# Two token tiles at a time in the down projection: seven products of quarters in place of eight

## The chip, the cores and the metric

The kernel runs on one core of a Trainium2 chip. The metric is device time in microseconds, the median of several executions. One further execution was recorded by the hardware profiler; the lines of profile in this document come from it. The engines are named PE (TensorE; PEld is its weight load), DVE (VectorE), ACT (ScalarE), POOL (GpSimd) and SP (SyncE, which here issues all the DMAs).

## The reference

1024 tokens of width 512 (two sequences of 512) go through four residual layers: a block-sparse linear layer, a gated FFN, a state-space mixer, and the same FFN with the same weights again. Each begins with a layer norm. The FFN, which is what the change touches:

```python
gate_proj = dequantize(gate_w, gate_s, gate_z, GROUP_SIZE, dt)   # 512 x 1792
up_proj = dequantize(up_w, up_s, up_z, GROUP_SIZE, dt)           # 512 x 1792
down_proj = dequantize(down_w, down_s, down_z, GROUP_SIZE, dt)   # 1792 x 512
gate = jax.nn.silu(jnp.dot(x, gate_proj))
up = jnp.dot(x, up_proj)
return jnp.dot(gate * up, down_proj)
```

`dequantize` subtracts a zero and multiplies by a scale, per group of 128 rows and per column. All is float32.

## The kernel before

Tokens come in eight tiles of 128 (`NT`), the width in four chunks of 128 (`KC`), the inner width 1792 in 14 chunks of 128 (`NFC`) or seven slabs of 256 (`NSLAB`). The residual stream `x_sb` stays in SBUF, tokens on the partitions; `xn_t` is the normed input, transposed. `h_t` holds silu(gate) * up transposed, inner width on the partitions, and `down` the dequantised down weights.

`ffn(which, first, waiting, after)` is called for both FFNs. Slab 0's gate and up products are plain (L417). From slab 1 on, each of the gate and up products of a slab is made by `seven` (L169): both the weights and the tokens are cut in two in both directions, and seven products of quarters replace eight (Strassen's scheme in Winograd's form). `seven` is a generator which the caller advances product by product, so that other work can be put between. Its seven products run in PSUM banks of tag `proj` for gate and `yo` for up, three banks each; the right-hand sums stand in `tq`, the left-hand ones are made on POOL by `left_sides` (L163 to L166). The sums of products are taken on DVE (L192, L197, L198, L206, L211), the gate's silu on ACT (L441) and the gating on DVE (L445). `tmp` is a ring of three SBUF tiles: for sums in the up product, and for normed tiles (`room`).

In each slab, the next slab's gate and up weights and this slab's down weights are dequantised (`dequant`, L225 to L231): three DMAs into `wi`, `zi`, `sf` (two buffers each), a subtraction on DVE (L230), and a product on POOL (L231). The down weights of slab s come behind five of the seven products of its up matrix:

```python
for _ in range(3):
    next(u)
dequant_down(s)
```

When all slabs are done, the down projection runs tile by tile, 14 matmuls of 128x128 by 128x512 each in one bank of tag `proj`, then an addition into `x_sb` on DVE (L474) and the callback `after(t, sg_tile)`. For the second FFN `after` stores the tile. For the first it is `to_mixer`: it stores the tile in DRAM (`x_d`), loads weights for the mixer, has the normed tile from two tiles ago transposed (`turn`, L134, with the copy to `xn_t` on ACT, L135), norms this tile (`norm`, L107 to L121), and for t = 5 begins the mixer's step sizes of the first sequence (`step_sizes`, `pd` on PE at L521), whose rest runs at t = 6 (L534 to L542).

Then the mixer begins: cumulated step sizes (`decays`: `pacs`, `pa`, `pl` on PE, which read `acs`), the last two tiles turned, the sums `two_quarters` (L145, L146) on DVE and `third_quarter`, `last_quarter` (L149, L156) on POOL, and the first products of `seven`.

The instructions of PE, ACT and DVE run in the order in which the program writes them. POOL and SP have their instructions ordered by a scheduler.

Of the kernel before, what the change touches and what calls it, by code (L numbers as in the profile page):

```python
# [8 lines left out]
F32 = mybir.dt.float32  # L9
# [5 lines left out]
P = 128  # L15
NTOK = 1024
NT = NTOK // P
SEQ = 512
NCH = SEQ // P
DIM = 512  # L20
KC = DIM // P
KH = KC // 2
# [7 lines left out]
NFC = FF // P  # L30
SLAB = 256
NSLAB = FF // SLAB
# [5 lines left out]
def kernel(  # L38
# [25 lines left out]
    nc = tc.nc  # L64
# [5 lines left out]
    psum = ctx.enter_context(tc.tile_pool(name="psum", bufs=2, space=bass.MemoryType.PSUM))  # L70


    x_sb = keep.tile([P, NT, DIM], F32, name="x_sb")
    xn_t = keep.tile([P, KC, NTOK], F32, name="xn_t")

    tq = keep.tile([P, 3, KH, SEQ], F32, name="tq")

    def room(*_):
        return keep.tile([P, SEQ], F32, tag="tmp", name="tmp", bufs=3)

    def weights():
# [10 lines left out]
        out=tri, in_=tri, compare_op=ALU.is_ge, fill=0.0, base=0, pattern=[[1, P]], channel_multiplier=-1  # L92
# [58 lines left out]
    def quarters():  # L151
        two_quarters()
        third_quarter()

    def last_quarter():
        nc.gpsimd.tensor_sub(B12, B22, B12)  # L156

    def left_sides(w):

        a11, a12, a21, a22 = w[:, :KH, 0], w[:, KH:, 0], w[:, :KH, 1], w[:, KH:, 1]  # L160
        sq = keep.tile([P, 3, KH, P], F32, tag="ws", name="ws", bufs=3)
        s1, s2, s4 = sq[:, 0], sq[:, 1], sq[:, 2]
        nc.gpsimd.tensor_add(s1, a21, a22)  # L163
        nc.gpsimd.tensor_sub(a21, a11, a21)
        nc.gpsimd.tensor_sub(s2, s1, a11)
        nc.gpsimd.tensor_sub(s4, a12, s2)  # L166
        return a11, a12, a21, a22, s1, s2, s4
# [54 lines left out]
    def dequant(dst, w, z, s, scratch, shape):  # L222

        wi, zi, sf = scratch
        nc.sync.dma_start(wi, w)  # L225
        nc.sync.dma_start(zi, z.partition_broadcast(P))
        nc.sync.dma_start(sf, s.partition_broadcast(P))

        def compute():
            nc.vector.tensor_tensor(dst, wi, zi, ALU.subtract)  # L230
            nc.gpsimd.tensor_tensor(dst, dst, sf, ALU.mult)  # L231

        return compute
# [30 lines left out]
    def now(q_compute):  # L264
        q, compute = q_compute
        compute()
        return q

    def dequant_gate(s, scratch):
        return dequant_in(s, gate_w, gate_z, gate_s, scratch)  # L270

    def dequant_up(s, scratch):
        return dequant_in(s, up_w, up_z, up_s, scratch)
# [102 lines left out]
        return first, [lambda n=n: lambda: turn(n) for n in waiting]  # L376


    def ffn(which, first, waiting, after):

        with tc.tile_pool(name=f"ffn{which}", bufs=1) as pool:
            h_t = pool.tile([P, NFC, NTOK], F32, name="h_t")
            down = pool.tile([P, NFC, DIM], F32, name="down")

            def scratch(shape):
                return [pool.tile(shape, ty, name=nm, bufs=2) for nm, ty in (("wi", I32), ("zi", I32), ("sf", F32))]

            def dequant_down(s):  # L390
                rows = slice(s * SLAB, (s + 1) * SLAB)
                grps = slice(s * (SLAB // P), (s + 1) * (SLAB // P))
                shape = [P, SLAB // P, DIM]
                dequant(
                    down[:, grps, :],
                    down_w[rows, :].rearrange("(j p) n -> p j n", p=P),
                    down_z[grps, :],
                    down_s[grps, :],
                    scratch(shape),
                    shape,  # L400
                )()

            def sg_tile(j, b):
                return pool.tile([P, SEQ], F32, tag=f"sg{j}{b}", name="sg")


            gq, uq = first
            for b in range(2):
                for j in range(2):
                    toks = slice(b * SEQ, (b + 1) * SEQ)  # L410
                    turns = [f() for f in waiting[:2]]
                    del waiting[:2]
                    pg = psum.tile([P, SEQ], F32, tag="proj", name="pg", bufs=3)
                    pu = psum.tile([P, SEQ], F32, tag="yo", name="pu", bufs=3)
                    for ps, q in ((pg, gq), (pu, uq)):
                        for kc in range(KC):
                            nc.tensor.matmul(  # L417
                                ps,
                                lhsT=q[:, kc, j, :],
                                rhs=xn_t[:, kc, toks],  # L420
                                start=(kc == 0),
                                stop=(kc == KC - 1),
                            )
                    sg = sg_tile(j, b)
                    nc.scalar.activation(sg, pg, AF.Silu)
                    nc.vector.tensor_mul(h_t[:, j, toks], sg, pu)
                    for f in turns:
                        f()
                if b == 0:
                    gq_next = left_sides(now(dequant_gate(1, scratch)))  # L430
                    quarters()
            last_quarter()
            uq_next = left_sides(now(dequant_up(1, scratch)))
            dequant_down(0)
            gq, uq = gq_next, uq_next
            for s in range(1, NSLAB):
                sgs = {(j, b): sg_tile(j, b) for j in range(2) for b in range(2)}
                more = s + 1 < NSLAB

                def gated(j, b, ps):  # L440
                    nc.scalar.activation(sgs[j, b], ps, AF.Silu)  # L441

                def times(j, b, ps):
                    toks = slice(b * SEQ, (b + 1) * SEQ)
                    nc.vector.tensor_mul(h_t[:, 2 * s + j, toks], sgs[j, b], ps)  # L445

                g = seven(gq, "proj", lambda j, b: sgs[j, b], gated, True)
                u = seven(uq, "yo", room, times, True)
                for _ in range(4):
                    next(g)  # L450
                if more:
                    gq = left_sides(now(dequant_gate(s + 1, scratch)))
                for _ in g:
                    pass
                for _ in range(2):
                    next(u)
                if more:
                    uq = left_sides(now(dequant_up(s + 1, scratch)))
                for _ in range(3):
                    next(u)  # L460
                dequant_down(s)
                for _ in u:
                    pass
            for t in range(NT):
                po = psum.tile([P, DIM], F32, tag="proj", name="ffn_o", bufs=3)
                for fc in range(NFC):
                    nc.tensor.matmul(  # L467
                        po,
                        lhsT=h_t[:, fc, t * P : (t + 1) * P],
                        rhs=down[:, fc, :],  # L470
                        start=(fc == 0),
                        stop=(fc == NFC - 1),
                    )
                nc.vector.tensor_add(x_sb[:, t, :], x_sb[:, t, :], po)  # L474
                after(t, sg_tile)

    def load_pair(*cts):

# [741 lines left out]
    with tc.manual_schedule(  # L1220
        engines={mybir.EngineType.PE, mybir.EngineType.Activation, mybir.EngineType.DVE}
    ):
        first, waiting = block_sparse()
        waiting_m = []

        state = {}

        def to_mixer(t, sg_tile):
            nc.sync.dma_start(x_d[t * P : (t + 1) * P, :], x_sb[:, t, :])
            if t == 0:  # L1230
                state["args"] = step_weights()
            if t in (1, 2):
                state[t] = load_pair(NCT, NCT + 1) if t == 1 else load_group(0)
            if len(waiting_m) == 2:
                turn(waiting_m.pop(0))
            waiting_m.append(norm_all(t))

            if t == NCH + 1:
                rooms = [sg_tile(*jb) for jb in ((0, 0), (0, 1), (1, 0))]
                state["steps"] = step_sizes(0, *state["args"], rooms)  # L1240
                next(state["steps"])
            if t == NCH + 2:
                for _ in state["steps"]:
                    pass

                nc.scalar.activation(small.tile([P, 1], F32, name="root"), eps, AF.Sqrt)

        ffn(0, first, waiting, to_mixer)
        first, waiting = mixer(waiting_m, state["args"], (state[1], state[2]))
        ffn(1, first, waiting, lambda t, _: nc.sync.dma_start(out[t * P : (t + 1) * P, :], x_sb[:, t, :]))  # L1250


# ---- launch: one core; numpy only lays the inputs out
# [46 lines left out]
```

## Time and profile before

| | before |
|---|---|
| median of 3 runs | 2308.8 us (2308.49 to 2309.22) |
| profiled execution, its time | 2307.23 us |
| its span in the profile | 2305.2 us |
| PE busy | 2288.9 us |
| DVE busy | 1608.5 us |
| ACT busy | 1158.3 us |
| POOL busy | 994.9 us |
| granted PE clock | 1.0 |

The span runs from the first to the last instruction; the execution's own time has some 2 us around it. Busy times are shares of the whole span; what a stage is limited by must be read in the stage. The first FFN has its seven slabs from 47 to 219.6 us and its down projection to 321.5 us; the mixer follows to about 2030 us; the second FFN's down projection begins at 2205.33 us.

A timeline line reads: start in us, duration in us, engine, line of the kernel, operation, output<-inputs with shapes, count, and in brackets the idle time before it and what ended it. A line of the chain reads: start, length, engine, tile and line, count.

### The profile page before, as it was taken

What the parts mean: (1) busy time and instruction counts of PE and PEld (TensorE: products, weight loads), DVE (VectorE), ACT (ScalarE), POOL (GpSimd) and SP (SyncE); (2) the same over time, 40 slices, a digit from 0 to 9 for tenths busy, and PEclk for the clock granted to TensorE, in tenths of its full rate; (3) what the DMA queues carried; (4) which work ended last, traced back from release to release, by engine and by line L of the source; (5) the groups of instructions that cost most, each with busy time, mean ns of one, the idle gap of its engine ahead of it and who ended that gap; (6) DMA issues with size and microseconds to landing.
All of it is one profiled execution on the core that took longest, in us unless ns stands there. A gap on an engine that the chain in (4) does not pass through costs nothing.

```text
span 2305.2 us, 27492 instructions
## 1 busy us (share of the span) xinstructions
PE 2288.9 (99%) x9680; PEld 1210.6 (53%) x9680; DVE 1608.5 (70%) x2816; ACT 1158.3 (50%) x2462; POOL 994.9 (43%) x965
## 2 busy tenths in 40 slices
PE   9999999999999999999999999999999999999999
PEld 5444454555555555555555555555555555544444
DVE  5454148887788787877877887878778788855510
ACT  4111046756665665666566656556665656521100
POOL 3764013444544454444445444444443543546500
PEclk9999999999999999999999999999999999999999
DMA  5663012222222222222222222222222222246500
GB/s 190 195 196 102 23 55 85 78 66 79 73 74 73 65 83 74 65 74 83 64 74 74 74 74 72 75 74 73 68 80 74 92 82 72 85 139 215 167 14 23
DMA packets 145769, 201.41 MB, mean 87 GB/s; under 512 B 7136, under 2 KB 92000, under 8 KB 145632
## 3 DMA queue, kind: packets, MB, share of 16 engines
q1 hardware_dynamic: 145632, 199.66, 27.1%
q8 instruction: 77, 1.26, 0.2%
q14 instruction: 60, 0.49, 0.1%
HBM read 194.91 MB, written 4.72 MB: 87 GB/s over the span
## 4 chain that ended last, share of the span: by engine, by line
PE 97%; DVE 2%; DMA 0%; ACT 0%; issue 0%; SPq 0%; DVEq 0%
PE proj L177 39%; PE po L827 19%; PE yo L177 10%; PE ffn_o L467 8%; PE py L793 5%; PE pst L725 4%; PE py L802 3%; PE x_tr L704 2%; PE pg L417 1%; PE pu L417 1%; PE bs_o L319 1%; PE pgm L655 1%; PE ln_tr L134 1%; DVE xc L611 0%; PE pd L521 0%
## 5 line engine op out<-in xcount | busy, mean ns | idle before, releaser
L780 POOL TENSOR_TENSOR ce<-ce,c_t 128x384 f32<-128x384 f32 x256 | 269.6, 1057 | 447.4 <-ACT ce L776 441.8
L827 PE MATMUL po<-wo,gt 128*128 128x512 f32 x992 | 436.8, 595 | 0.0
L177 PE MATMUL proj<-xn_t,w 128*128 128x512 f32 x912 | 424.8, 596 | 0.5 <-DVE gt L206 0.5
L766 ACT ACTIVATE m<-bc,acs 128x128 f32<-128x128 f32 x1024 | 324.5, 389 | 4.4 <-PE py L793 4.4
L827 PEld LDWEIGHTS po<-wo,gt 128*128 128x128 f32 x992 | 184.6, 190 | 219.6 <-issue 193.9
L177 PE MATMUL proj<-tq,ws 128*128 128x512 f32 x608 | 278.8, 592 | 1.3 <-DVE xc L611 1.3
L177 PEld LDWEIGHTS proj<-xn_t,w 128*128 128x128 f32 x912 | 165.7, 190 | 179.5 <-issue 171.8
L774 DVE TENSOR_TENSOR m<-m,gm 128x512 f32<-128x512 f32 x256 | 220.9, 883 | 0.4 <-ACT m L773 0.4
L611 DVE SCALAR_TENSOR_TENSOR xc<-proj,cw,xc 128x511 f32<-128x511 f32 (+2 forms) x288 | 213.6, 742 | 2.5
L163 POOL TENSOR_TENSOR ws<-w 128x256 f32<-128x256 f32 x96 | 72.1, 752 | 331.7 <-DMA w<-in_win_t_dram 329.4
L467 PE MATMUL ffn_o<-down,h_t 128*128 128x512 f32 x448 | 193.4, 592 | 0.0
L712 POOL TENSOR_TENSOR x_dec<-x_dt,dec 128x384 f32<-128x384 f32 x128 | 129.9, 1025 | 128.2 <-DVE x_dt L708 122.2
L820 POOL TENSOR_TENSOR sq_acc<-sq_acc,y 128x512 f32<-128x512 f32 x128 | 176.0, 1389 | 13.8 <-ACT y L819 13.6
L177 PEld LDWEIGHTS proj<-tq,ws 128*128 128x128 f32 x608 | 112.8, 190 | 131.6 <-issue 122.2
L837 DVE TENSOR_TENSOR x_sb<-x_sb,po 128x512 f32<-128x512 f32 x248 | 168.0, 678 | 19.8 <-PE po L827 17.8
L793 PE MATMUL py<-m,x_dt 128*64 128x128 f32 x2048 | 180.8, 276 | 0.1
L773 ACT ACTIVATE m<-m 128x512 f32<-128x512 f32 x256 | 161.3, 630 | 7.4
L608 ACT ACTIVATE xc<-proj,cb,cw 128x512 f32<-128x512 f32 x96 | 71.3, 775 | 164.5 <-DVE proj L206 146.5
L802 PE MATMUL py<-ce,state 128*64 128x128 f32 x1536 | 149.4, 273 | 0.0
L177 PE MATMUL proj<-tq,w 128*128 128x512 f32 x304 | 143.0, 592 | 0.8 <-DVE gt L197 0.8
L177 PE MATMUL proj<-xn_t,ws 128*128 128x512 f32 x304 | 142.8, 592 | 0.0
L467 PEld LDWEIGHTS ffn_o<-down,h_t 128*128 128x128 f32 x448 | 84.7, 190 | 104.8 <-issue 104.8
(178 smaller groups left out, 3429.0 us busy)
## 6 DMA issues: line engine op xcount, KB each, us to landing
bc<-acs_d SPq DMA_DIRECT2D x128, 512.0 KB, 3.7
w<-in_win_t_dram SPq DMA_DIRECT2D x64, 512.0 KB, 3.8
wo<-in_wo_t_dram SPq DMA_DIRECT2D x31, 512.0 KB, 3.7
wi<-in_down_w_dram SPq DMA_DIRECT2D x14, 512.0 KB, 3.9
zi<-in_down_z_dram SPq DMA_DIRECT2D x14, 512.0 KB, 4.8
sf<-in_down_s_dram SPq DMA_DIRECT2D x14, 512.0 KB, 4.1
wi<-in_gate_w_dram SPq DMA_DIRECT2D x13, 512.0 KB, 3.9
zi<-in_gate_z_dram SPq DMA_DIRECT2D x13, 512.0 KB, 4.9
```

Source lines behind the costliest of these rows:

```text
L177: nc.tensor.matmul(ps, lhsT=a[:, kc, :], rhs=b[:, kc, :], start=(start and kc == 0), stop=(stop and kc == KH - 1), skip_group_check=True,)
L467: nc.tensor.matmul(po, lhsT=h_t[:, fc, t * P : (t + 1) * P], rhs=down[:, fc, :], start=(fc == 0), stop=(fc == NFC - 1),)
L611: nc.vector.scalar_tensor_tensor(dst[:, s:], ps[:, : SEQ - s], cw[:, t, 3 - s : 4 - s], dst[:, s:], ALU.mult, ALU.add)
L766: nc.scalar.activation(m[:, c, :], bc[:, hh, c * P : (c + 1) * P], AF.Relu, bias=acs[:, t, h : h + 1], scale=-1.0,)
L773: nc.scalar.activation(m, m, AF.Exp, scale=-1.0)
L774: mults.append(lambda: nc.vector.tensor_mul(m, m, shared[b][2]))
L780: nc.gpsimd.tensor_mul(ce, ce, c_t[:, P:].rearrange("p (c l) -> p c l", l=P))
L793: nc.tensor.matmul(py[hh * HD : (hh + 1) * HD, c * P : (c + 1) * P], lhsT=x_dt[:, c, hh, :], rhs=m[:, c, :], start=True, stop=(c == 0),)
L802: nc.tensor.matmul(py[hh * HD : (hh + 1) * HD, c * P : (c + 1) * P], lhsT=state[:, c - 1, hh, :], rhs=ce[:, c - 1, :], start=False, stop=True,
L820: nc.gpsimd.tensor_add(sq_acc[:, b, :], sq_acc[:, b, :], y)
L827: nc.tensor.matmul(po, lhsT=gts[j, b][:, c * P : (c + 1) * P], rhs=wo[:, j, :], start=(j == 0), stop=(j == PP - 1),)
L837: nc.vector.tensor_add(acc[:, t, :], acc[:, t, :], po)
```

## The change

The down projection takes two token tiles at once. The left matrix (256 tokens by 1792) is cut in two by tiles and in two by halves of the inner width (7 chunks each, `KF`), and `down` in two by the same halves and in two by halves of the 512 columns (`DH` = 256). Seven products of quarters, each 7 matmuls of 128x128 by 128x256, are made for each of the four pairs.

- The weight sums: `quarter1` = b12 - b11 on POOL behind slab 4's down weights (`first_right`); b12 becomes b22 - b12 in place, on POOL, five chunks behind slab 5's down weights and two in slab 6 (`third_right`); b22 - `quarter1` on DVE in the up product of slab 6, into `tq` (`second_right`); b21 less that, on DVE in the first pair, into the rest of `tq` and one `sg` tile (`fourth_right`).
- The token sums, `left_side`, on DVE: for the first pair in slab 6 (chunks of the slabs so far behind the second up product, the other two chunks after the slab loop), for each later pair in the middle of the pair before it.
- In slab 6 the down weights are dequantised at the start of the slab.
- In a pair the first two products (`v`, `w`) have banks of tag `proj`. `v` is copied to an SBUF tile (`m1`) by ACT and added from there to all four output quarters. `y` accumulates three products and `z` two, in banks of tag `yo`; each is read and added to an output quarter after each of its products, before the next accumulates on it.
- `after` is called for the even tile before the last product of the pair is issued, for the odd tile behind it. The rest of the step sizes moves from `to_mixer` to a new callback `within`, called in the last pair behind the sixth addition.

The diff:

```diff
-    def ffn(which, first, waiting, after):
+    def ffn(which, first, waiting, after, within):
...
+            KF, DH = NFC // 2, DIM // 2
+            quarter1 = pool.tile([P, KF, DH], F32, name="quarter1")
+            flat = tq.rearrange("p i k s -> p (i k s)").rearrange("p (k n) -> p k n", n=DH)
+            NQ4 = 3 * KH * SEQ // DH - KF
+            spare = []
+            b11, b12 = down[:, :KF, :DH], down[:, :KF, DH:]
+            b21, b22 = down[:, KF:, :DH], down[:, KF:, DH:]
+
+            def first_right():
+                nc.gpsimd.tensor_sub(quarter1, b12, b11)
+
+            def third_right(ks):
+                nc.gpsimd.tensor_sub(b12[:, ks], b22[:, ks], b12[:, ks])
+
+            def second_right():
+                nc.vector.tensor_sub(flat[:, :KF], b22, quarter1)
+
+            def fourth_right():
+                spare.append(sg_tile(1, 1).rearrange("p (k n) -> p k n", n=DH))
+                for out, ks in ((flat[:, KF:], slice(0, NQ4)), (spare[0], slice(NQ4, KF))):
+                    nc.vector.tensor_sub(out, b21[:, ks], flat[:, ks])
+
+            def q4(k):
+                return flat[:, KF + k, :] if k < NQ4 else spare[0][:, k - NQ4, :]
+
+            def left_tiles():
+                return [pool.tile([P, KF, P], F32, tag=tag, name="lq", bufs=2) for tag in ("wi", "zi", "sf")]
+
+            def left_side(u, tiles, k0=0, k1=KF):
+                c0, c1 = slice(2 * u * P, (2 * u + 1) * P), slice((2 * u + 1) * P, (2 * u + 2) * P)
+                ks, ks2 = slice(k0, k1), slice(KF + k0, KF + k1)
+                a11, a12, a21, a22 = h_t[:, ks, c0], h_t[:, ks2, c0], h_t[:, ks, c1], h_t[:, ks2, c1]
+                s1, s2, s4 = [q[:, ks] for q in tiles]
+                nc.vector.tensor_add(s1, a21, a22)
+                nc.vector.tensor_sub(s2, s1, a11)
+                nc.vector.tensor_sub(a21, a11, a21)
+                nc.vector.tensor_sub(s4, a12, s2)
...
+                if not more:
+                    dequant_down(s)
+                    third_right(slice(KF - 2, KF))
...
-                for _ in range(3):
+                if not more:
+                    lefts = left_tiles()
+                    left_side(0, lefts, 0, KF - 2)
+                next(u)
+                if not more:
+                    second_right()
+                for _ in range(2):
                     next(u)
-                dequant_down(s)
+                if more:
+                    dequant_down(s)
+                if s == KF // 2 + 1:
+                    first_right()
+                if s == NSLAB - 2:
+                    third_right(slice(0, KF - 2))
                 for _ in u:
                     pass
-            for t in range(NT):
-                po = psum.tile([P, DIM], F32, tag="proj", name="ffn_o", bufs=3)
-                for fc in range(NFC):
-                    nc.tensor.matmul(
-                        po,
-                        lhsT=h_t[:, fc, t * P : (t + 1) * P],
-                        rhs=down[:, fc, :],
-                        start=(fc == 0),
-                        stop=(fc == NFC - 1),
...
-                nc.vector.tensor_add(x_sb[:, t, :], x_sb[:, t, :], po)
-                after(t, sg_tile)
+            left_side(0, lefts, KF - 2, KF)
+            lo, hi = slice(0, DH), slice(DH, DIM)
+
+            def ffn_o(tag):
+                return psum.tile([P, DH], F32, tag=tag, name="ffn_o", bufs=3)
+
+            def product(ps, a, b, start, stop):
+                for k in range(KF):
+                    nc.tensor.matmul(
+                        ps,
+                        lhsT=a[:, k, :],
+                        rhs=b(k),
+                        start=(start and k == 0),
+                        stop=(stop and k == KF - 1),
+                        skip_group_check=True,
+                    )
+
+            def add(t, cols, v):
+                nc.vector.tensor_add(x_sb[:, t, cols], x_sb[:, t, cols], v)
+
+            for u in range(NT // 2):
+                v, w, y, z = [ffn_o(tag) for tag in ("proj", "proj", "yo", "yo")]
+                t0, t1 = 2 * u, 2 * u + 1
+                s1, s2, s4 = lefts
+                a11, a12 = h_t[:, :KF, t0 * P : t1 * P], h_t[:, KF:, t0 * P : t1 * P]
+                s3, a22 = h_t[:, :KF, t1 * P : (t1 + 1) * P], h_t[:, KF:, t1 * P : (t1 + 1) * P]
+                product(v, a11, lambda k: b11[:, k, :], True, True)
+                m1 = room()[:, :DH]
+                nc.scalar.copy(m1, v)
+                product(w, a12, lambda k: b21[:, k, :], True, True)
+                for t, cols in ((t0, hi), (t1, hi), (t1, lo), (t0, lo)):
+                    add(t, cols, m1)
+                add(t0, lo, w)
+                product(y, s2, lambda k: flat[:, k, :], True, False)
+                if u == 0:
+                    fourth_right()
+                add(t0, hi, y)
+                product(z, s1, lambda k: quarter1[:, k, :], True, False)
+                if u + 1 < NT // 2:
+                    lefts = left_tiles()
+                    left_side(u + 1, lefts)
+                add(t1, hi, z)
+                product(y, s3, lambda k: b12[:, k, :], False, False)
+                add(t1, hi, y)
+                within(u)
+                product(z, s4, lambda k: b22[:, k, :], False, True)
+                add(t0, hi, z)
+                after(t0, sg_tile)
+                product(y, a22, q4, False, True)
+                add(t1, lo, y)
+                after(t1, sg_tile)
...
-            if t == NCH + 2:
+
+        def rest_of_steps(u):
+            if u == NT // 2 - 1:
                 for _ in state["steps"]:
                     pass
 
                 nc.scalar.activation(small.tile([P, 1], F32, name="root"), eps, AF.Sqrt)
 
-        ffn(0, first, waiting, to_mixer)
+        ffn(0, first, waiting, to_mixer, rest_of_steps)
...
-        ffn(1, first, waiting, lambda t, _: nc.sync.dma_start(out[t * P : (t + 1) * P, :], x_sb[:, t, :]))
+        ffn(1, first, waiting, lambda t, _: nc.sync.dma_start(out[t * P : (t + 1) * P, :], x_sb[:, t, :]), lambda u: None)
```

## The prediction

> **What bounds the kernel now.** I read the page's busy row and clock first, then the chain that ended last, then the chain and the timelines of the stretch that the change rewrites.
>
> ```profile
> span 2305.2 us, 27492 instructions
> PE 2288.9 (99%) x9680; PEld 1210.6 (53%) x9680; DVE 1608.5 (70%) x2816; ACT 1158.3 (50%) x2462; POOL 994.9 (43%) x965
> ...
> PE 97%; DVE 2%; DMA 0%; ACT 0%; issue 0%; SPq 0%; DVEq 0%
> ```
>
> PE is 97% of the chain. A busy PE need not be PE at its peak, so what counts is the spacing of its instructions. The chain in order of time over the end of the kernel, and in the first FFN's tail, gives it:
>
> ```profile
> 2193.31 12.02 PE yo L177 x28
> 2205.33 96.15 PE ffn_o L467 x224
> 2301.47 0.02 issue
> 2301.50 0.69 DVE x_sb L474
> ```
>
> ```profile
> 321.52 0.44 PE ln_tr L134 x4
> 321.96 0.89 PE pacs L578 x8
> 322.85 0.86 PE pa L589 x2
> 323.71 0.86 PE pl L590 x2
> 324.57 0.44 PE ln_tr L134 x4
> 325.00 1.72 PE proj L177 x4
> 326.72 0.44 PE ln_tr L134 x4
> 327.16 3.57 PE pd L521 x32
> ```
>
> A down projection is 224 records (a float32 product is two) without a gap, 96.15/224 = 0.4292 us each for 512 columns. The 128-wide `pd` records come every 3.57/32 = 0.1116 us. So PE alone sets the time of both down projections, and the seam to the mixer has no gap either: each step there is ready just in time.
>
> [...]
>
> ```profile
> 167.46 0.73 POOL L163 TENSOR_TENSOR ws<-w 128x256 f32<-128x256 f32 x1
> 168.27 1.06 POOL L164 TENSOR_TENSOR w<-w 128x256 f32<-128x256 f32 x1
> ```
>
> L164 alone takes 0.72; here VectorE's L445 (two SBUF inputs, asking from 167.88) went in ahead of it and itself took 0.85 in place of 0.69. The waiting VectorE instruction won against POOL's next.
>
> **The change, part by part.**
>
> *PE work.* Per FFN, 4 pairs x 7 products x 7 chunks x 2 records = 392 records of 256 columns replace 224 of 512. No row shows 256 columns. On the line through 0.1116 (128) and 0.4292 (512) they cost 0.2175 us[...]. I take 0.2175: 85.3 us, 10.9 less than 96.15[...]. Two FFNs: **-21.8**[...]. A weight load shows as 190 ns, shorter than a record; and loads of the same size keep up with `pd`'s 0.1116 spacing, so I charge none.
>
> *Weight sums on GpSimd.* A row of 1024 columns takes 2.35 us there, so `first_right` (1792) takes 4.1, `third_right` 2.9 and 1.2. In slab 4 POOL is free from the end of the down dequantisation (174.18) to the next gate (181.13): 6.9 us hold the 4.1. `third_right` falls into slab 6, where no weights of this FFN remain. Cost 0 under those gaps. `dequant_down(6)` moves to the start of slab 6: its three DMAs keep their place in SP's queue (issued 188.96 to 191.44, landing in 4 to 5 us, thus ready at 196), and behind them stand only the mixer's weights, due after 325. Its VectorE subtraction (1.22) precedes the first PSUM sum of the slab, which PE gives out at 199.0. POOL's multiply ends at 198.2, VectorE gets the port then (as above), done 199.4: the sum is 0.3 late, used 1.7 later. Cost 0. If POOL's `third_right` got the port first, the sum would end at 203.0, and PE, wanting that bank at 200.7, would lose 2.3 in each FFN.
>
> *Token sums in slab 6.* Here I see a new wait. Before, in the second FFN (timelines of VectorE and PE):
>
> ```profile
> 2196.85 0.69 DVE L192 TENSOR_TENSOR tmp<-tmp,yo 128x512 f32<-128x512 f32 x1 [2.81 <-PE yo L177]
> 2200.22 0.69 DVE L197 TENSOR_TENSOR tmp<-tmp,yo 128x512 f32<-128x512 f32 x1 [2.67 <-PE yo L177]
> ...
> 2201.73 1.88 PE L177 MATMUL yo<-tq,w 128*128 128x512 f32 x4
> ```
>
> Between L192 and L197 the change queues `left_side` on 640 columns (four times 0.82, 3.25 with their overlap) and `second_right` on 1792 (2.02). The gap was 2.67. L197 then ends at 2197.54 + 3.25 + 2.02 + 0.69 = 2203.5, less some 0.1 of overlap, where it had ended at 2200.9. PE's sixth product accumulates on the bank that L197 reads and wants it at 2201.73: **+1.7**. Everything later on VectorE (L198, the gatings, the 256-column rest of `left_side`) is late too, but ends some 3.5 before PE needs it, since the first two new products (6.1 us) use neither; they have banks of tag `proj`, free since the gate. In the first FFN, POOL forms the mixer's left sides then (209.95 to 212.98, 0.73 each), and the port costs VectorE about 1.1 more: **+2.8**. Together +4.5; from 1 to 7, since the widths are priced and not seen.
>
> *The pair loop.* A product is 14 x 0.2175 = 3.05 us, a pair 21.3. VectorE per pair: ten adds of 256 (0.42) = 4.2, `left_side` on 896 columns 4 x 1.09 = 4.4, two norms 4.0; `fourth_right` 2.1 in pair 0. It is busy under two thirds. Tightest place: `y` ends at 9.1, its add at 9.6, `left_side` at 13.9, the add of `z` at 14.3, and PE wants `z` again at 15.2. Margin 0.9; POOL is idle then, so nothing stretches it. `fourth_right` ends at 8.6 of 9.1. The `m1` copy on ACT lies under the next product. Cost 0; if the margins fail, up to 1 a pair.
>
> *The seam to the mixer.* The rest of the step sizes ran at 312.5 to 318.6, under token tile 7's products. Now `within` puts it after the first half of `y` in the last pair. With T as this pair's start: y's add ends 15.6, two VectorE steps, Ln and Exp with the table load between (0.63 + 1.28 + 0.63), four VectorE steps at 0.72: `acs` at T+21.6. Behind it on VectorE wait the add of `z` (22.0), norm 6 (24.1), the last add, norm 7 (26.5). PE finishes both transposes at 22.2, and runs `pacs`, `pa`, `pl` to 24.8, turns 6, projects, and can turn 7 at 26.9. So these just fit. ACT, in its order, copies `pacs` only after norm 7's root, so the copies of `pa` and of tiles 6 and 7 slip; `pd` starts 0.2 late, `two_quarters` ends about 1 later against it, and GpSimd's L149 and L156 behind it deliver the fourth mixer product's operand about 0.6 late. Before, L156 ended at 333.5 for a product due at 334.2. The mixer's opening is a VectorE chain (L197 at 335.92 onward), so this stays lost: **+0.8**, from 0 to 3. x_d's last two stores move behind those adds, and `acs_d`'s store 0.7 later on SP; its readers come about 10 us after.
>
> *The end.* The last add is 256 columns: 0.42 for 0.69, **-0.25**. Its output DMA is as before.
>
> Sum: -21.8 + 4.5 + 0.8 - 0.25 = **-16.8** on the profiled execution's 2307.2 (2.0 around its span). The median of the runs, 2308.8, is 1.6 higher; I carry the difference over: **2292.0**. A difference of 0.2% (4.6 us) is about what the measurement can tell from none.
>
> **Rivals.**
>
> *VectorE keeps up after all* (shorter widths run faster than priced, the seam holds): -21.8 to -23.0 and -0.25, so 2286. For it: five of the six edits have cover. Against: a 2.67 gap doesn't hold 5.3 us of work. Chance 0.2.
>
> *VectorE and GpSimd become the local bound*: POOL takes the port at slab 6 (2 x 2.3), the seam costs 3, two pairs lose 0.5 each: 7.8 more, 2300. For it: all margins are under 1 us. Against: L445 above took the port from a waiting POOL. Chance 0.2.
>
> *PE's weight load shows at 256 columns, and the kernel is slower.* The change raises loads from 448 to 784. If half of a 190 ns load came between records, they would cost 0.3125 us, 392 of them 122.5: +26 in each FFN, with the stalls 2366. It decides from the spacing at which 784 records plus 5.1 of stalls equal 192.3: 0.239 us, 10% above my price. Against it stand `pd`'s 0.1116. Chance 0.05, with anything else unforeseen that costs so much.
>
> The sum as worked out: 0.55. Of the middle cases a few end near no gain.
>
> **How the numbers follow.** Likeliest 2292. The fast rival at 2285.5 is the low end; the high end takes the local-bound rival nearly whole, 2300. Faster by over 0.2%: 0.92; within: 0.03; slower: 0.05.
>
> **What would show it.** Right: `ffn_o` spacing of 0.2175 in the chain; in slab 6's `yo` stretch a VectorE link (`second_right`, L424 of the changed kernel, and L197) of 1.7 and 2.8; no gap in pairs 0 to 3; VectorE and POOL links near the seam. Wrong: record spacing over 0.22; a gap between `z` and its second product; a link through `third_right` (L421) or L230 at the start of slab 6.

## The result, and the profile after

| | before | after |
|---|---|---|
| median of four runs each, side by side | 2308.68 us (2308.49 to 2309.22) | 2290.74 us (2289.07 to 2292.84) |
| ratio, 95% interval | 1 | 0.9922 (0.9905 to 0.9940) |
| profiled execution, its time | 2307.23 us | 2289.07 us |
| its span | 2305.2 us | 2287.0 us |
| PE busy | 2288.9 us | 2266.9 us |
| DVE busy | 1608.5 us | 1676.6 us |
| granted PE clock | 1.0 | 1.0 |

The kernel became 0.8% faster. The page of the changed kernel, its span, busy row and the shares of the chain:

```profile
span 2287.0 us, 28312 instructions
PE 2266.9 (99%) x10016; PEld 1274.1 (56%) x10016; DVE 1676.6 (73%) x2926; ACT 1159.5 (51%) x2469; POOL 1014.3 (44%) x971
...
PE 95%; DVE 2%; DMA 1%; ACT 1%; issue 0%; SPq 0%; DVEq 0%; ACTq 0%
```

PE is busy 22.0 us less and the span is 18.2 shorter: some 4 us were given back as waits. The chain in order of time, over the same stretch as before (the up product of slab 6 in the second FFN, then its down projection), shows both:

```profile
2185.35 3.45 PE yo L177 x8
...
2188.89 0.69 DVE tmp L192
2189.58 0.75 DVE lq L443
...
2190.35 0.84 DVE lq L444
...
2191.83 0.82 DVE lq L446
2192.65 1.94 DVE tq L424
2194.58 0.61 DVE tmp L197
...
2195.24 3.70 PE yo L177 x8
2198.93 84.62 PE ffn_o L529 x392
```

The down projection is one piece of 392 records without a gap: 84.62/392 = 0.2159 us each, where 224 had taken 96.15. Ahead of it the chain, which ran over PE alone before, now leaves PE for L192, passes through `left_side` (L443 to L446), `second_right` (L424) and L197, and returns at 2195.24. From the first `yo` to the first `ffn_o` it is 13.58 us where it had been 12.02: 1.56 of wait. In the first FFN the same piece runs from 208.46 to 222.60, that is 14.14: 2.12 of wait. PE's timeline there names the same instruction:

```profile
218.90 1.98 PE L177 MATMUL yo<-tq,w 128*128 128x512 f32 x4 [1.85 <-DVE tmp L197]
```

The seam to the mixer, first in the chain, then in PE's timeline:

```profile
313.41 0.89 PE pacs L674 x8
...
318.61 3.63 PE pd L617 x32
```

```profile
325.98 3.70 PE L177 MATMUL proj<-xn_t,w 128*128 128x512 f32 x8 [0.30 <-POOL xn_t L156]
...
337.66 3.70 PE L177 MATMUL yo<-tq,ws 128*128 128x512 f32 x8 [0.22 <-ACT acs L687]
```

The last of these waits is not new. Before, it was longer:

```profile
345.76 3.70 PE L177 MATMUL yo<-tq,ws 128*128 128x512 f32 x8 [0.40 <-ACT acs L591]
```

`pd` needs 3.63 in place of 3.57, and the fourth mixer product waits 0.30 for GpSimd's L156, where nothing waited before. The later wait for ACT's copy of `acs` shrinks from 0.40 to 0.22. From the start of `pacs` to this `yo` it is 24.25 us; before it was 23.80 (321.96 to 345.76).

Stretch by stretch along the chain, after less before:

| stretch | before | after | difference |
|---|---|---|---|
| start to the first `seven` | 75.42 | 76.28 | +0.86 |
| first FFN, slabs 1 to 6 | 144.20 | 146.32 | +2.12 |
| its down projection (without turns and `pd`) | 96.13 | 84.60 | -11.53 |
| seam, `pacs` to the mixer's first long `yo` | 23.80 | 24.25 | +0.45 |
| mixer, and slab 0 of the second FFN | 1715.37 | 1715.51 | +0.14 |
| second FFN, slabs 1 to 6 | 144.20 | 145.76 | +1.56 |
| its down projection | 96.15 | 84.62 | -11.53 |
| end | 3.73 | 3.44 | -0.29 |

The sum is -18.2. The first line lies ahead of every changed instruction, and it differs between executions: in two further profiles of kernels with the same opening, also at a clock of 1.0 (steps_back and steps_early, below), it is 75.32 and 76.86. So the 0.86 says nothing of the change.

### The profile page after: what moved, and what is told of

Its sections match the earlier page's. It is cut to its first block, busy times and chain, and to the rows that moved or that the text cites. A ratio compares the mean times of both kernels' runs of the same rounds, so it can differ in the third digit from the quotient of the medians.

```text
span 2287.0 us, 28312 instructions
## 1 busy us (share of the span) xinstructions
PE 2266.9 (99%) x10016; PEld 1274.1 (56%) x10016; DVE 1676.6 (73%) x2926; ACT 1159.5 (51%) x2469; POOL 1014.3 (44%) x971
## 4 chain that ended last, share of the span: by engine, by line
PE 95%; DVE 2%; DMA 1%; ACT 1%; issue 0%; SPq 0%; DVEq 0%; ACTq 0%
PE proj L177 39%; PE po L923 19%; PE yo L177 10%; PE ffn_o L529 7%; PE py L889 5%; PE pst L821 4%; PE py L898 3%; PE x_tr L800 2%; PE pg L459 1%; PE pu L459 1%; PE bs_o L319 1%; PE pgm L751 1%; PE ln_tr L134 1%; DVE xc L707 0%; PE pd L617 0%; DMA wi<-in_up_w_dram 0%
## 5 line engine op out<-in xcount | busy, mean ns | idle before, releaser
L889 PEld LDWEIGHTS py<-m,x_dt 128*64 128x64 f32 x2048 | 122.5, 137 | 29.1 <-issue 19.7
L189 ACT COPY gt<-proj 128x512 f32<-128x512 f32 x32 | 18.8, 586 | 227.3 <-PE proj L177 227.1
```

Of the source, the lines that this page charges most:

```text
L889: nc.tensor.matmul(py[hh * HD : (hh + 1) * HD, c * P : (c + 1) * P], lhsT=x_dt[:, c, hh, :], rhs=m[:, c, :], start=True, stop=(c == 0),)
```

## The experiments

Each kernel was run beside the kernel before. The first four shared one chip (before there: 2308.61, 2306.93 to 2310.34), the last four another (before: 2308.41, 2307.08 to 2309.91). My theory was the prediction's: PE's records give the gain, slab 6 and the seam take some back, the pair loop nothing. The rivals: the pair loop has hidden costs; the weight load or the 256-column form has a price of its own; the seam is not what its move was priced at. Where the prediction and an expectation speak of the port, they mean what the prediction's rows show: instructions of VectorE and GpSimd that meet take longer (L445 0.85 us for 0.69, L164 1.06 for 0.72). What lies behind it was not shown.

**The changed kernel again (after_again).** No edit.

> The changed kernel once more, as the yardstick for the other runs. Theory (the gain is the narrower work of PE; losses are the wait in slab 6, about 3.5 us in both FFNs, and 0.5 at the seam to the mixer): median within 2 us of 2290.7, ffn_o spacing 0.2159 us again. Its four executions so far spread over 3.8 us (2289.1 to 2292.8) where the kernel before spreads over 0.7, with granted PE clocks of 0.998 to 1.0. If the slower ones are a moment of a lower granted clock, an execution with a clock below 1.0 shows it in one stretch of the profile; if they are the opening DMAs, the stretch up to the first gate product differs (47.9 us here, 47.1 before).

Measured: 2290.13 us (2288.48 to 2291.53), ratio 0.9917 (0.9902 to 0.9932). Down projection 84.62 again; the waits of slab 6 are 1.97 and 1.57. The result stands, and the waits came again in a second profile, so they are not those of one execution. The opening is where the two profiles differ, and there the clock does too (the last section).

**One part of the queue in slab 6 moved (second_late).** `second_right` goes behind the slab loop:

```diff
                 next(u)
-                if not more:
-                    second_right()
                 for _ in range(2):
                     next(u)
...
             left_side(0, lefts, KF - 2, KF)
+            second_right()
```

> One edit: second_right is issued behind the slab loop and the last token sums, no longer between the third and fourth product of the last up matrix. Theory (the new wait in slab 6 is VectorE's queue: 3.25 us of left_side plus 2.02 of second_right in a gap of 2.7): left_side alone just fits, so PE's gap before the sixth up product goes from 2.0 and 1.5 us to 0 to 0.2, and nothing else waits, since the first two products of the pair (6 us) cover second_right: 3.2 to 3.5 us faster than the changed kernel. Rival (the wait is for GpSimd's port or for the weights, and moves along): the gap stays or comes back before the third product of pair 0, no change in time.

Measured: 2287.04 us (2286.11 to 2287.99), ratio 0.9904 (0.9889 to 0.9919); its runs and those of after_again don't overlap, and the medians lie 3.1 apart (3.2 to 3.5 expected). Its chain over the same stretch of the second FFN:

```profile
2185.74 12.02 PE yo L177 x28
2197.76 84.62 PE ffn_o L528 x392
```

The DVE link is gone and the up product is back at 12.02. In the first FFN 0.24 is left of it. Against the expectation something else waits there, in the middle of the first pair, where the moved 2 us now stand (PE's timeline):

```profile
238.10 3.29 PE L528 MATMUL ffn_o<-down,lq 128*128 128x256 f32 x14 [0.58 <-DVE x_sb L538]
```

So the wait of slab 6 was the queue on DVE ahead of L197, as the theory has it. The new 0.58 says that the first pair of the first FFN has no 2 us to spare.

**The other part moved (left_early).** `left_side` on five chunks goes from behind the up product's second step to the end of the gate product:

```diff
                 for _ in g:
                     pass
+                if not more:
+                    lefts = left_tiles()
+                    left_side(0, lefts, 0, KF - 2)
                 for _ in range(2):
                     next(u)
                 if more:
                     uq = left_sides(now(dequant_up(s + 1, scratch)))
-                if not more:
-                    lefts = left_tiles()
-                    left_side(0, lefts, 0, KF - 2)
```

> One edit, the other half: left_side on 640 columns is issued at the end of the last gate product, before the first sum of the up product; second_right stays. Theory (VectorE's queue[...]): second FFN no gap before the sixth up product; first FFN, where GpSimd forms the mixer's left sides at that moment, left_side stretches from 3.25 to 4 to 4.7 and a gap of up to 1 us appears before the fourth up product. Rival (it is second_right's own wait, for PE's third product or the weights): the gaps of 2.0 and 1.5 stay.

Measured: 2287.54 us in its single run, span 2285.5. The second FFN's `yo` piece is 12.02 again; in the first, PE waits 0.35 for L192, since two of the four left-side instructions take 1.34 in place of 0.82 (all four: 4.1), where the expectation puts POOL's left sides for the mixer (in the changed kernel's profile these run from 210.67 to 214.16). Either part of the queue, moved alone, removes the wait of the second FFN and most of that of the first. Slab 6 and the pairs of the first FFN together keep 0.60 us of loss with this edit and 1.07 with the other.

**The 256-column record by itself (before_halves).** The kernel before, each tile's product made in two halves of 256 columns, 448 records an FFN with the same arithmetic:

```diff
-                po = psum.tile([P, DIM], F32, tag="proj", name="ffn_o", bufs=3)
-                for fc in range(NFC):
...
-                        rhs=down[:, fc, :],
...
-                nc.vector.tensor_add(x_sb[:, t, :], x_sb[:, t, :], po)
+                for cols in (slice(0, DIM // 2), slice(DIM // 2, DIM)):
+                    po = psum.tile([P, DIM // 2], F32, tag="proj", name="ffn_o", bufs=3)
+                    for fc in range(NFC):
...
+                            rhs=down[:, fc, cols],
...
+                    nc.vector.tensor_add(x_sb[:, t, cols], x_sb[:, t, cols], po)
```

> The kernel before, with each token tile's down projection made in two column halves of 256 (28 matmuls of 128x256 in place of 14 of 128x512): the same arithmetic, twice the weight loads, no products saved. Theory (256 columns cost 0.2159 us a record, no weight load shows): 448 records take 96.7 us in each FFN where 224 took 96.15; 1 to 1.5 us slower than before in all, less some tenths for the narrower last addition. Rival (weight loads at 256 columns are not free): 0.239 us and more a record, 107 us and more, over 20 us slower. If denser weight loads lower the granted clock, it shows here as well: clocks of 0.998 to 0.999 and a spread of some us.

Measured: 2310.82 us (2308.38 to 2312.23), ratio 1.0008 (0.9999 to 1.0017). The chain of its second FFN:

```profile
2207.68 96.71 PE ffn_o L468 x448
```

96.71/448 = 0.2159 us, again; twice the weight loads cost 96.71 - 96.15 = 0.56 us an FFN. No more of the load shows: a short record takes 1.3 ns more than half of a long one (429.2/2 = 214.6). With it the slower rival of the prediction is out, in a kernel with none of the other edits. Nor do the denser loads show in the clock or the spread: its runs have clocks of 0.999 to 1.0 and spread over 3.9 us, those of the kernel before beside it 0.999 to 1.0 and 3.4 us. The medians lie 2.2 us apart for the 1 to 1.5 expected, but the interval takes in no difference at all.

**The step sizes earlier (steps_early).** The rest of the step sizes in two halves: the first behind the add of `w`, the second behind the first add of `z`, both in the last pair.

```diff
                 add(t0, lo, w)
+                within(u)
...
                 add(t1, hi, z)
+                within(u)
                 product(y, s3, lambda k: b12[:, k, :], False, False)
                 add(t1, hi, y)
-                within(u)
...
             if u == NT // 2 - 1:
+                if "half" not in state:
+                    state["half"] = True
+                    next(state["steps"])
+                    return
                 for _ in state["steps"]:
```

> One edit to the changed kernel: in the last pair of the first FFN the rest of the step sizes is issued in two halves, behind the addition of w and behind the first addition of z, where VectorE waits for PE anyway. Theory (at the seam VectorE's queue, step sizes then two norms then two_quarters, is what makes GpSimd's L156 and so the fourth mixer product late): acs some 5 us earlier, norms done when their tiles are, and the gap of 0.3 us before the fourth product goes, as does most of the 0.4 that the mixer's opening then loses on VectorE; the seam from the last ffn_o to the first yo product of the mixer shortens from 24.25 us to 23.8, as before the change. Rival (L156 is late for another reason, as GpSimd's own queue): the gap stays.

Measured: 2289.18 us in its single run, span 2287.1; its seam must be read by itself, since its opening was longer too. From `pacs` (314.02) to the long `yo` (337.56) it is 23.54 us: 0.7 less than after, 0.3 less than before. The chain there is PE again where the changed kernel left it for DVE and ACT, and the wait for L156 is gone:

```profile
319.23 3.57 PE pd L618 x32
322.80 10.30 PE proj L177 x24
```

This is one profile, but the seam varies little: in the five profiles with the step sizes behind the sixth addition (after, after_again, second_late, left_early and left_more) it is 24.16 to 24.25, and in best, the other one with this edit, 23.72. So the seam's loss came from where the step sizes were put, and it can be had back.

**The step sizes where they were (steps_back).** In `to_mixer` at t = 6, with `within` empty:

```diff
+            if t == NCH + 2:
+                for _ in state["steps"]:
+                    pass
+
+                nc.scalar.activation(small.tile([P, 1], F32, name="root"), eps, AF.Sqrt)
...
         def rest_of_steps(u):
-            if u == NT // 2 - 1:
-                for _ in state["steps"]:
-                    pass
-
-                nc.scalar.activation(small.tile([P, 1], F32, name="root"), eps, AF.Sqrt)
+            pass
```

> One edit to the changed kernel, its last part undone: the rest of the step sizes goes back to to_mixer at token tile 6, behind that tile's norm. Theory (the seam's order on VectorE decides): acs is ready only about 4.5 us after PE has turned tile 5, so PE waits 3 to 4.5 us before pacs; the seam of 24.25 us becomes 27 to 29. Rival (VectorE has slack there, PE's own 2.6 us of pacs, pa and pl cover it): under 1 us.

Measured: 2295.18 us in its single run, span 2293.1. PE's timeline at the seam:

```profile
318.17 2.05 PE L674 MATMUL pacs<-tri,acs 128*128 128x128 f32 x8 [5.75 <-DVE acs L638]
```

The wait is of the kind expected and larger: 5.75 for 3 to 4.5. With it the seam is 31.5 us (312.41 to 343.89), 7.2 more than in the changed kernel and beyond the 27 to 29 expected. And behind it `pacs` and `pa` take 3.6 on the chain for 1.75, which no theory of mine had. The busy time of PE in stretches tells why (the columns are the stretch, its length, PE busy and its records, granted clock, DMA share, GB/s):

```profile
318.10:319.20 1.10, 1.03 (x5) 0.50 0.29 108
319.20:320.20 1.00, 1.00 (x6) 0.50 1.00 373
320.20:321.80 1.60, 1.60 (x4) 0.59 0.57 213
321.80:324.00 2.20, 2.20 (x9) 1.00 0.28 104
```

Behind the wait the granted clock is 0.50, until about 321.5 by an estimate from the mean of 0.59 in the third stretch, so for some 3 us; from 321.80 on it is 1.00. The 1.9 us that `pacs` and `pa` lose there come on top of the wait: in PE's timeline `pacs` takes 2.05 us, where the later `pacs` of the same form, at 338.94, takes 1.05. The pair calls back for tile 6 only one product before its end, so the move to `within` is not a by-product: without it the seam would have taken back 7 more of the 18 us.

**The pair loop's margin (left_more).** `left_side` of the later pairs gets two more subtractions of 896 columns on DVE, which repeat the last one:

```diff
                     left_side(u + 1, lefts)
+                    for _ in range(2):
+                        nc.vector.tensor_sub(lefts[2], h_t[:, KF:, 2 * (u + 1) * P : (2 * u + 3) * P], lefts[1])
```

> The pair loop's cover measured: behind each left_side in the pair loop its last subtraction (896 columns, 1.0 to 1.1 us) is repeated twice, same operands, same result. Theory (the tightest place of a pair is the add of z before its second product, with about 1 us to spare): 2.1 us more leave PE waiting 1.0 to 1.2 us in each of the first three pairs of both FFNs, 6 to 7 us in all, and nothing in the fourth, which has no left_side. Rival (VectorE, busy under two thirds, has room for it): no gaps and no time.

Measured: 2299.81 us in its single run, span 2298.1. PE's timeline, pair 0 of the first FFN:

```profile
241.26 3.29 PE L529 MATMUL ffn_o<-down,lq 128*128 128x256 f32 x14 [1.19 <-DVE x_sb L539]
```

The same gap of 1.19 stands before the second product of `z` in pairs 0 to 2 of both FFNs, and none in pair 3, which prepares no left side. 2.2 us of added work (1.10 and 1.09) give 1.2 of gap: the margin of the changed kernel is 1.0, at the place that the prediction named. On the chain a gap costs more than its idle time: the second FFN's down projection is 2205.66 to 2294.63, 88.97 for 84.62, so 1.45 each and 8.7 for all six, not 6 to 7, because a product that restarts is slower in its first record (483 ns for 379) and the idle time is counted from the end of the product before it, whose 3.19 us are 0.17 more than 14 spacings of 0.2159. The other 2.4 of the 11.1 us of span lie ahead of the first pair.

**Both repairs (best).** The edits of left_early and steps_early together.

> Two edits to the changed kernel at once: left_side of the first pair at the end of the last gate product (as in the run before), and the step sizes in two halves (as in this call). Theory: the gaps of 2.0 and 1.5 us go but for 0.35 in the first FFN, the seam gives back 0.4: 3.5 us faster than the changed kernel, 2286.6 at its 2290.1, ratio to the kernel before 0.9905. Rival (the two interact, since earlier VectorE work meets other work): less than 2 us.

Measured: 2286.72 us (2286.36 to 2287.22), ratio 0.9906 (0.9889 to 0.9922), 4.0 below the changed kernel's median (3.5 expected), and all its runs are below all of the changed kernel's, in the first measurement and in after_again. They are not clear of those of second_late (2286.11 to 2287.99), which has one repair alone. The seam is 312.99 to 336.71, 23.72; the end of the second FFN has no DVE link left:

```profile
2184.25 12.02 PE yo L177 x28
2196.27 84.62 PE ffn_o L529 x392
```

This version beats the kernel before and the changed one.

## Why the prediction was right, point by point

Its term for PE and its term for slab 6 were both somewhat too careful, and the others were small: -23.06 for PE, +3.68 for the two waits, +0.45 for the seam and -0.29 for the end make -19.2 along the chain, for -16.8 predicted. The 0.86 of the opening and 0.14 of the mixer, which no term foresaw, bring it to the -18.2 of the spans. That the three misses were partly offset there is luck. So is the last step: the 1.6 us carried from the profile to the median came out at 1.67, in four runs that spread over 3.8.

*PE work.* Right in kind, mis-sized. The line through 128 and 512 columns priced the record of 256 at 0.2175 us. It took 0.2159 in the changed kernel, in its second run and in before_halves, 1.3 ns more than half of the long record's 429.2. 392 times 0.0016 is 0.6 us an FFN. The -23.0 of the fast rival was an estimate of mine; PE's work came to -23.06.

*Weight sums on GpSimd.* The cost of nothing holds, but one place was misread. `first_right` is written behind slab 4's down weights, and I looked for its cover there. GpSimd's order is the scheduler's, and it needs only chunks 0 to 6, so it ran behind slab 3's (POOL's timeline):

```profile
151.09 3.97 POOL L418 TENSOR_TENSOR quarter<-down 128x1792 f32<-128x1792 f32 x1
157.96 2.35 POOL L231 TENSOR_TENSOR w<-w,sf 128x1024 f32<-128x1024 f32 x1 [2.91 <-PE proj L177]
```

2.91 us stay free behind it; 3.97 measured for 4.1 estimated. In slab 6 VectorE went first again, as L445 does in the trace of before, and against the local-bound rival (timelines of POOL and of DVE):

```profile
196.72 2.35 POOL L231 TENSOR_TENSOR down<-down,sf 128x1024 f32<-128x1024 f32 x1
199.15 3.75 POOL L421 TENSOR_TENSOR down<-down 128x1280 f32<-128x1280 f32 x1
```

```profile
197.94 2.22 DVE L230 TENSOR_TENSOR down<-wi,zi 128x1024 f32<-128x1024 int32 x1
200.08 0.67 DVE L192 TENSOR_TENSOR sg<-sg,proj 128x512 f32<-128x512 f32 x1
```

DVE's L230 starts at 197.94 and takes 2.22 in place of 1.21; POOL's multiply ends at 199.07. `third_right` starts on POOL at 199.15 and ends 3.75 later, where the 2.35 of 1024 columns give an estimate of 2.9 for its 1280; L230 finishes in the first 1.0 of that, at 200.16. So the waiting DVE instruction had gone first. PE lost nothing.

*Token sums in slab 6.* The place, the chain of causes and the second FFN's size (1.56 for 1.7) were right, shown by second_late and left_early. The first FFN's 2.12 for 2.8 fails in one term: I charged 1.1 for meeting POOL's left sides, and only two instructions were longer.

```profile
212.61 0.96 DVE L443 TENSOR_TENSOR lq<-h_t 128x640 f32<-128x640 f32 x1
213.60 1.24 DVE L444 TENSOR_TENSOR lq<-lq,h_t 128x640 f32<-128x640 f32 x1
```

0.14 and 0.42 over the 0.82 that the other two of the four take: 0.56.

*The pair loop.* No gap in any of the eight pairs. The prediction's sum for VectorE is under two thirds of a pair only without `fourth_right`; with it, pair 0 of the first FFN comes to 14.7 of 21.3 us. The margin came out at 1.0 for 0.9 (the add of `z` ends at 2212.92, its next product starts at 2213.88), and left_more shows that it is this place that binds. POOL is idle there, as the prediction said, but not in the whole pair: in pair 0 of the first FFN it forms left sides for the mixer from 225.5 to 228.8, and the four adds of `m1` take

```profile
226.06 3.06 DVE L539 TENSOR_TENSOR x_sb<-x_sb,tmp 128x256 f32<-128x256 f32 x4 [0.54 <-ACT tmp L549]
```

in place of some 1.4 in the second FFN. It cost PE nothing here. The prediction had no such term; second_late, which puts 2 us more there, has a gap of 0.58.

*The seam.* +0.8 predicted, +0.45 measured. Of the links that were named, L156 carries it: the fourth product waits 0.30, for 0.6 predicted. `pd`, said to start 0.2 late, starts 5.20 us behind `pacs` as before and only takes 0.06 longer, and the wait for ACT's copy of `acs` became shorter. The late step sizes cause the loss: steps_early takes it back.

*The rivals.* That DVE keeps up falls with the two waits; second_late and left_early get near its 2286 only once the queue is taken apart. The local bound falls with the order in slab 6 (L230 done at 200.16, `third_right` at 202.90) and the gapless pairs; the weight load with before_halves.

## What to carry to other kernels

When a product scheme trades matmuls for sums, price the matmul by its measured spacing, and then look for the stretch where all of the first sums must be made at once: here the narrower records gave 23 us, and waits took back 3.7 in one slab, behind the in-order queue of one engine, and 0.45 at the seam. An instruction that is needed late must not be written ahead of one that PE waits for; moving either half of the queue was worth some 3 us. Of a margin of 1 us under PE, say which instruction holds it and test it by adding work there, since the next edit will use it up.

## What the runs showed of the hardware

- A float32 matmul record of 256 columns comes every 215.9 ns (84.62 us for 392 in the changed kernel, 96.71 for 448 in before_halves), half of 512's 429.2 and 1.3 more. Weight loads take 190 ns each, one for each record; in before_halves twice as many of them cost 0.56 us an FFN.
- VectorE took 0.42 us for 256 columns, 0.82 for 640, 1.09 for 896, 1.49 for 1280 and 2.02 for 1792. The prediction had priced the widths but 1280, at the same figures. The line through two widths in the profile of before, 0.689 at 512 (L474) and 1.219 at 1024 (L145), gives as estimates 0.42, 0.82, 1.09, 1.48 and 2.01.
- PE's clock after a wait: 0.50 for some 3 us behind 5.75 us without work in steps_back. The longest wait of PE in the parts that the change touches is 1.85 us, in slab 6 of the first FFN of the changed kernel, and there (214.7 to 222.6) the granted clock is 1.0.
- The granted clock between 20 and 48 us of the span was 1.0 in four of the ten profiles and 0.94 in the other six. There PE waits for the first layer's tiles (0.46 and 1.39 us near 21 us), and in left_more the eight `bs_o` records behind these waits took 5.30 us, in steps_back 3.60. In the second run of the changed kernel, with 0.94, the up product of slab 6 began 1.65 us later than in the first. 28 us at 0.94 do the work of 26.3 at 1.0, so by this estimate the low clock accounts for 1.7 of the 1 to 4 us by which executions of one kernel differ here. What brings it about is open: the same two waits stand in the profiles with 1.0, so they alone don't decide it, and nothing here tested it.
